# A deeper convolution pipeline in the head and four staggered lanes in the tail of a scan kernel

## The chip, the cores and the metric

The kernel runs on one core of one Trainium2 chip. The metric is the device time of one execution in microseconds (us). Each kernel was run several times and profiled once. Every run told here is of the fast state. A difference counts as faster or slower from 2% up; below that the verdict is "same", and smaller effects are read from stages of the profile.

Engines: PE is the matrix engine TensorE (PEld its weight loads), DVE is VectorE, ACT is ScalarE, POOL is GpSimd, SP is the engine that issues most DMAs; "SPq" is a DMA issue in SP's queue.

## The reference, cut to what matters

Four images of 64 × 64 × 96 go through one block (projection, convolution, selective scan in four directions) and then one layer of linear attention and a feed-forward net.

```python
xz = bilinear(x, W_in, s_in, b_in)              # sign(x) @ sign(W).T * scale
xp, z = jnp.split(xz, 2, axis=-1)
t = conv3x3(sign(xp + move0_b), sign(conv_W) * mean|conv_W|)
t = prelu(t + conv_b + rp_b0) + rp_b1 + xp
u = silu(t)                                      # 192 channels, 4096 points
# four directions: rows, columns, and both reversed
dts, Bs, Cs = split(bilinear(u in the direction, Wl, ...))
h = exp(delta * A) * h + delta * u * B           # 16 states per channel, step by step
y = sum(h * C) + D * u
# ... the four directions summed, layer norm, gate silu(z), projection; then
# attention (one 96 x 96 matrix per image, known only once all of it is summed), FFN
```

## The kernel before

The program has three stages. The **head** makes the weights' signs, convolves the first image in 16 parts, forms B, C and delta ("row stage", "start"). The **scan** runs 1536 pieces and takes the other images' heads along. The **tail** finishes the last image in lanes: sums and norms (three lanes), the 96 × 96 matrix ("middle"), the rest (`last`, four lanes).

Work is written as generators; `interleave` advances each by one step and so sets the order in every engine's queue. The instructions of an engine run in that order in these traces: in part 2 below, u is ready at 67.7 us and starts at 74.4, behind two casts in DVE's queue.

```python
def run(c):                                     # head
    made, first = c.weights(), prologue(c, 0, c.xts)
    ...
    while (0, 1) not in c.ready:
        interleave([made, first])               # one weights step, one prologue step
        c.later.tick()                          # stores that are due go to SP

# convolution, one part, two deep: matmuls of part n, all else of part n-1
for s in range(4):
    ...4 or 3 matmuls of part n into cv; the projection ahead at s = 0 and 2...
    if prev:
        if s == 0: cz = cz*s + v; cz = cz + r*oma          # DVE twice
        elif s == 1: sign(...); e = exp(-cz)               # ACT twice
        elif s == 2: e = ln(1+e); e = exp(-e)              # ACT twice
        elif s == 3: u = cz*e; store u; by_columns(u)      # DVE, SP; POOL turns it
v = cv*acs + acb                                           # DVE
r = relu(cv*csc + cbias)                                   # ACT, same bank
cz = winT.T @ xsT                                          # PE

def sign(h, q, pz):
    ...
    for m in range(3):
        c.later.store(xgw[...], sg[m::3, :])               # SP

# scan.start(): loads of utd and bc are issued here
nc.sync.dma_start(v[0], ud[0:128, 0:16])                   # 512 KB of utd first
for q in range(NQ):
    self.load_bc(0, self.bt, 0, 0, 0, q)                   # then 2 MB of bc
for x in range(2): ...                                     # then 256 KB of utd

# tail
drain([e.middle()])
drain([e.last(ln) for ln in [e.lane] + more])              # four lanes in lockstep
```

Here sg, v, r, e and u take turns on eight tiles of one pool, five tiles to a part: a tile is free for its next owner only when the store that reads it has landed. (... cut: everything of the scan, and the branches for images after the first.)

## Time and profile before

5479.21 us in the median of its first runs, 5478.45 over those of the comparison with the change. The stages are cut at visible events of the timeline: first convolution matmul, last sign, first copy of the row stage, first and last scan, first matmul with the finished matrix.

| stage of before | from | to | us |
|---|---|---|---|
| weights and projection | 0 | 56.2 | 56.2 |
| convolution to its last sign | 56.2 | 173.5 | 117.3 |
| hand-over to the row stage | 173.5 | 188.3 | 14.8 |
| row stage | 188.3 | 211.1 | 22.9 |
| delta and the first loads | 211.1 | 237.7 | 26.6 |
| scan | 237.7 | 5355.5 | 5117.8 |
| tail up to the matrix | 5355.5 | 5407.5 | 52.0 |
| `last` in four lanes | 5407.5 | 5482.3 | 74.8 |

The lines that carry this reading stand in the prediction. The table is for the time between two events on different engines, which no single view prints: take both starts from the timeline and subtract.

### The profile page before, as it was taken

The numbers are of one execution on the slowest core, as the hardware profiler recorded it, in microseconds if no ns is written. First come the engines' busy times: TensorE is split into PE (matmuls) and PEld (weight loads), VectorE is DVE, ScalarE is ACT, GpSimd is POOL, SyncE is SP. The second block draws the span as 40 slices with busy tenths as digits, with TensorE's granted clock in tenths as the row PEclk, the third lists the DMA queues.
The fourth block names the chain that finished last, engine by engine and source line by source line (L and its number), as shares of the span: only waits on it lengthen the run. The fifth ranks groups of instructions, "written<-read, shape, count | busy, mean of one in ns | idle before, by whom it ended". The sixth has DMA issues, their size and how long they took to land. (4 is left out here: it accounts for less than half of the span.)

```text
span 5482.3 us, 62080 instructions
## 1 busy us (share of the span) xinstructions
PE 3415.9 (62%) x20083; PEld 1355.4 (25%) x20083; DVE 5016.3 (91%) x3171; ACT 3615.3 (66%) x5648; POOL 4938.7 (90%) x2245
## 2 busy tenths in 40 slices
PE   6456665467656776657764676664676664444577
PEld 3222222122222222222222222221232221111233
DVE  4499999899999999999999999999999999999994
ACT  4467777687766667778777666776666775555554
POOL 2399999899999999999999999999999999999990
PEclk7666776678766777767886787766787666666777
DMA  4565666767666666576665665667666565665652
GB/s 82 128 211 171 207 207 199 228 213 213 195 200 201 189 208 204 196 244 213 217 199 181 216 198 186 216 192 225 217 218 187 189 204 194 195 211 194 212 175 62
DMA packets 624219, 1069.06 MB, mean 195 GB/s; under 512 B 237307, under 2 KB 355092, under 8 KB 622100
## 3 DMA queue, kind: packets, MB, share of 16 engines
q1 hardware_dynamic: 623236, 1065.07, 62.2%
q8 instruction: 157, 2.57, 0.2%
q14 instruction: 170, 1.39, 0.1%
q10 hardware_dynamic: 656, 0.02, 0.0%
HBM read 830.01 MB, written 228.56 MB: 193 GB/s over the span
## 5 line engine op out<-in xcount | busy, mean ns | idle before, releaser
L423 POOL TENSOR_TENSOR w<-dl,bc 128x1024 f32<-128x1024 f32 x1524 | 3550.0, 2355 | 88.0 <-PE yp L1462 52.8
L1389 ACT ACTIVATE dA<-dl,anm 128x1024 f32<-128x1024 f32 x1524 | 1701.1, 1116 | 486.0 <-DVE w L423 284.5
L423 DVE TENSOR_TENSOR_SCAN dA<-dA,cy,w 128x1024 f32<-128x1024 f32 x725 | 1698.6, 2343 | 107.8 <-ACT dA L1389 94.2
L423 POOL TENSOR_TENSOR w<-h,bc 128x1024 f32<-128x1024 f32 x570 | 1341.4, 2353 | 127.8 <-DVE h L423 113.6
L1462 PE MATMUL yp<-w,sum 128*32 128x256 f32 x12288 | 1254.7, 505 | 323.8 <-ACT pd L1343 235.0
L423 DVE TENSOR_TENSOR w<-dA,bc 128x1024 f32<-128x1024 f32 x966 | 1183.1, 1225 | 65.4 <-DMA bc<-bcd 4.0
L423 DVE TENSOR_TENSOR_SCAN h<-dA,cy,w 128x1024 f32<-128x1024 f32 x427 | 999.2, 2340 | 17.4 <-ACT dA L1389 16.7
L1462 PEld LDWEIGHTS yp<-w,sum 128*32 128x32 f32 x12288 | 316.9, 127 | 1401.0 <-issue 731.4
L1431 ACT COPY cy<-dA 128x1 f32<-128x1 f32 x725 | 114.0, 157 | 753.2 <-DVE w L423 751.3
L423 DVE TENSOR_TENSOR_SCAN dA<-dA,w 128x1024 f32<-128x1024 f32 x241 | 550.2, 2283 | 34.7 <-ACT dA L1389 28.0
L1324 PE MATMUL dps<-gT,wdz 128*128 128x64 fp8e5 x1008 | 116.6, 316 | 399.9 <-ACT ys L1476 373.9
L423 DVE TENSOR_TENSOR_SCAN h<-dA,w 128x1024 f32<-128x1024 f32 x143 | 325.9, 2279 | 18.8 <-POOL w L423 16.1
L1337 PE MATMUL dps<-sp,ident 128*128 128x512 f32 x378 | 268.5, 799 | 96.2 <-ACT dps L1333 96.1
L1467 PE MATMUL yp<-ya,back 128*128 128x256 f32 x576 | 226.3, 511 | 0.0
L682 PE MATMUL cv<-tp,cwA 128*96 128x512 fp8e5 x576 | 197.9, 467 | 33.3 <-ACT r L729 30.9
L1324 PEld LDWEIGHTS <-wdz 128*128 128x128 fp8e5 x1008 | 95.6, 153 | 479.2 <-issue 451.7
L1324 PE MATMUL dps<-gT,wdy 128*128 128x64 fp8e5 x504 | 58.7, 318 | 221.0 <-ACT ys L1476 220.8
L1431 ACT COPY cy<-h 128x1 f32<-128x1 f32 x427 | 79.3, 186 | 133.5 <-DVE h L423 132.8
L994 PE MATMUL yc<-eys,mean 96*96 96x512 f32 x240 | 141.4, 744 | 29.5 <-DVE vks L423 14.4
L1329 ACT ACTIVATE pd<-dps,dbias,pvd 128x512 f32<-128x512 f32 x189 | 143.9, 761 | 20.8 <-PE dps L1324 20.5
L1467 PEld LDWEIGHTS yp<-ya,back 128*128 128x128 f32 x576 | 117.6, 236 | 119.9 <-issue 88.2
L1330 ACT ACTIVATE sp<-dps,dbias,pvd 128x512 f32<-128x512 f32 x189 | 144.8, 766 | 0.0
(363 smaller groups left out, 4457.2 us busy)
## 6 DMA issues: line engine op xcount, KB each, us to landing
dl<-dld SPq DMA_DIRECT2D x762, 512.0 KB
bc<-bcd SPq DMA_DIRECT2D x512, 512.0 KB
dld<-pd SPq DMA_DIRECT2D x126, 512.0 KB
yd<-ys SPq DMA_DIRECT2D x768, 64.0 KB
dld<-pd SPq DMA_DIRECT2D x126, 256.0 KB
ya<-yd SPq DMA_DIRECT2D x192, 128.0 KB
pu<-ud SPq DMA_DIRECT2D x32, 512.0 KB
pu<-utd SPq DMA_DIRECT2D x31, 512.0 KB
```

Source lines behind the costliest of these rows:

```text
L423: return getattr(self.eng, name)(out, *args, **kw)
L682: nc.tensor.matmul(ps, w[:, 96 * h : 96 * h + 96], tp[:, 8 * q + dy : 8 * q + dy + 8, dx : dx + IW], start=(w is taps[0][1]), stop=(w is t ...
L994: self.c.nc.tensor.matmul(ps, w, x, start=(i == 0), stop=(i == len(pairs) - 1))
L1324: nc.tensor.matmul(pv[:, s], wd[:, k, s], gT[:, :, c0 : c0 + 16], start=(s == 0), stop=(s == 7))
L1329: nc.scalar.activation(d[:, 0], ps, AF.Abs, scale=sc, bias=bi)
L1330: nc.scalar.activation(t, ps, AF.Relu, scale=sc, bias=bi)
L1337: nc.tensor.matmul(ps, c.ident, t, start=False, stop=True, skip_group_check=True)
L1389: c.nc.scalar.activation(t, self.dlt[i // NQ][0], AF.Exp, scale=c.anm[:, g, NQ * KORD[e] + q : NQ * KORD[e] + q + 1])
L1431: self.c.nc.scalar.copy(self.carries[g, q], h[:, CH - 1 : CH])
L1462: c.nc.tensor.matmul(y[32 * x : 32 * x + 32, g % 2, :], c.sum4, prod[:, 256 * x : 256 * x + 256], start=(q == 0), stop=(q == NQ - 1 and no ...
L1467: c.nc.tensor.matmul(y[:, g % 2, :], w, src, start=False, stop=(n == len(more) - 1))
```

## The change

Its intent: keep all engines busy in the convolution by working on three parts at once, take away waits for memory and for DMA around it, and let the four lanes of the tail use different engines at the same time. The diff, cut to its core (pool names, the weights' `scales` block, the reversed order in which the tail takes its columns, and unchanged branches left out):

```diff
+    next(made)
     while (0, 1) not in c.ready:
-        interleave(lanes)
+        interleave([first])                    # weights only every second step
         c.later.tick()
+        if (0, 1) not in c.ready:
+            interleave(lanes)
+            c.later.tick()
...
-                per = 2 if alone and h else 4  # u turned: 64- or 128-byte runs
+                per = 2 if alone else 4        # 64-byte runs, tiles of the scan's pool
...
+                    if alone and q == NQ8 - 1:
+                        held.append((dst, ut)) # last two stores after the last part
-                    c.later.store(xgw[...], sg[m::3, :])
+                    if alone:
+                        nc.gpsimd.dma_start(dst, sg[m::3, :])
...
+            def alone_parts():                 # conv n, sign/exp n-1, Ln/Exp/u n-2
...
+                if fast and j % 4 > 1:         # row stage: four banks
+                    return c.p.ps.tile([128, 512], F32, ..., tag=f"y{j % 2}")
...
                     nc.sync.dma_start(gw[:, x, 16:64], ...sgd...)
+                    if fast and x:
+                        c.loads_ahead()        # bc x4, then utd
...
+        if i == len(self.pieces) - 1:
+            self.last_ys = t                   # last y read from its tile
+            return
...
+    last = [e.last(ln) for ln in [e.lane] + more]
+    for g in last:
+        next(g)                                # first loads ahead of the matrix
     drain([e.middle()])
-    drain([e.last(ln) for ln in [e.lane] + more])
+    drain([apart(2 * x, g) for x, g in enumerate(last)])
```

## The prediction

> **What bounds the kernel now.** I read the page's busy row and its 40 slices first, then a table of windows with edges at visible events (start of the convolution, the first row-stage copy, the first scan, the last scan), then the waits of the first 240 us, the timeline of one convolution part, and the chain that ended last.
>
> The page, busy row and two slices:
>
> ```profile
> PE 3415.9 (62%) x20083; PEld 1355.4 (25%) x20083; DVE 5016.3 (91%) x3171; ACT 3615.3 (66%) x5648; POOL 4938.7 (90%) x2245
> ...
> DVE  4499999899999999999999999999999999999994
> ...
> POOL 2399999899999999999999999999999999999990
> ```
>
> DVE and POOL are full in slices 3 to 39 and half idle in the first two and the last. The windows say so with times (start:end, length, busy of PE, PEld, DVE, ACT, POOL, PE clock, DMA share, GB/s):
>
> ```profile
> 13.00:41.50 28.50, 12.83 (x62) 8.08 (x61) 13.96 (x34) 11.03 (x27) 12.42 (x39) 0.53 0.70 86
> ...
> 77.00:110.00 33.00, 23.44 (x93) 11.78 (x92) 12.39 (x17) 22.13 (x36) 4.23 (x4) 0.95 0.52 67
> 110.00:145.00 35.00, 26.98 (x96) 13.16 (x95) 14.56 (x20) 22.51 (x36) 5.29 (x5) 0.85 0.47 87
> ...
> 177.00:188.00 11.00, 1.05 (x8) 0.93 (x9) 0.00 (x0) 0.00 (x0) 0.81 (x1) 0.50 0.73 102
> ...
> 237.70:5350.00 5112.30, 3183.78 (x19064) 1237.10 (x19065) 4864.77 (x2903) 3442.40 (x5363) 4890.02 (x2131) 0.72 0.64 203
> ...
> 5405.00:5482.00 77.00, 58.79 (x195) 24.97 (x194) 37.97 (x73) 38.69 (x65) 0.00 (x0) 0.74 0.22 62
> ```
>
> So there are three stages: a head of 237.7 us, a scan of about 5119 us at 95% of DVE and 96% of POOL, and a tail of about 125 us. The change hardly touches the scan's instructions. At most 363 us are therefore open to it, and 2% of the whole is 109.6 us: nearly a third of head and tail together.
>
> The waits of the head show a serial chain rather than a busy engine:
>
> ```profile
> DVE u L423 <- ACT e L713: 54.5, 15, 4.6
> ACT r L729 <- DVE v L726: 29.7, 16, 4.3
> ...
> PE xa L760 <- DMA xg<-sg: 15.3, 1, 15.3
> ACT xr L765 <- DMA utd<-ut: 12.3, 1, 12.3
> ```
>
> One part of the convolution, from the timeline (only the starts matter): v 104.32, r 105.15, second multiply-add 106.08, sign 106.91, exp 107.40, tp 107.88, sz 108.54, Ln 109.21, Exp 109.87, u 110.53, next v 111.14. That is 6.82 us in which DVE and ACT take turns. The fourth row above is a buffer: the row copies reuse memory of the u tiles, so they wait until the stores of u have landed, at 188.25, although the matmul they read had started at 181.97.
>
> The tail's chain walks all four lanes through each operation together (start, us):
>
> ```profile
> 5408.83 5.98 DMA l4t<-td
> 5414.94 1.99 PE l4ps L994 x2
> ...
> 5430.35 0.70 DVE h L1218
> 5431.08 0.36 DVE h L1219
> 5431.46 0.43 DVE h L1220
> ```
>
> First DMA alone, then PE alone, then ACT alone, then DVE alone from 5430 to 5437.
>
> **What the Trainium skill says.** (1) "TensorE: Matmul & The Clock Gate", Part 1 (the HAM clock gate): TensorE runs at 1.2 GHz until about 3.4 us of sustained work have passed, then at 2.4; a 512-column matmul starts every 426.7 ns cold and every 215.7 ns warm. The trace agrees: weight loads of the convolution are 0.43 us apart near 105, and six of its matmuls near 110.7 take 1.46 us; the window 77 to 110 has clock 0.95, 177 to 213 has 0.50. (2) "PSUM — Partial Sum Buffer", "PSUM bank collisions raise a hardware error": engines have to be kept out of one bank and quadrant at once, readers too. The trace agrees in form: r waits for v 16 times, 29.7 us, though both only read cv. (3) "DMA: Bandwidth & Descriptors", "Issuing engines are not separate DMA queues": issuing from another engine saves only sequencer time. The same page's specifications give a first byte of about 1 us from GpSimd against 0.6 from SP. The page of before has no queue of GpSimd's, so no run yet shows it; three SP issues of sg take 1.77 us in the timeline.
>
> **The change part by part.**
>
> *Weights ahead of and inside the convolution.* Before, everything of the weights is made by 56.1. The window 13 to 41.5 has DVE 14, ACT 11, POOL 12.4, PE 12.8 of 28.5 us busy, with a 9.0 us wait of the first projection matmul for xb behind DVE's reduces. The change moves those reduces behind it, interleaves weights with the eight xb/project steps, and starts the convolution with 15 weight steps to come. The reduces' wait (about 8) and the stretch after the projects (41.6 to 56.1, of which half stays) give 15: convolution from 41. Given back: 8 fp8 transposes and casts at about 1.2 us on DVE (10), some small DVE work (5), and two POOL items of 4.1, over parts 0 to 5.
>
> *Three parts deep.* A part then costs its busiest engine, not the 6.82 chain. ACT by issue intervals: sign 0.49, exp 0.48, Ln 0.66, Exp 0.66, r 0.66, tp 0.66 (1.33 where it comes in two halves), sz 0.67: 4.28 to 4.95 with the next image row's projection, 2.95 without. DVE: v 0.80, two multiply-adds 1.5, u 0.69: 3.0, plus weights 2.5 in parts 0 to 5. PE: 18 matmuls by 0.22 = 4.0 warm, or by 0.43 = 7.7 cold. I take 6.5 for six parts (DVE with weights, order of queues), 4.7 for six, 3.7 for four and 6.5 for draining: 39+28+15+6.5 = 88.5, last sign at 129.5, against 173.5. Cumulative gain 44, of which 15 from the start and 29 from the parts (56.1 to 173.5 was 117.4).
>
> *sg by GpSimd, u tiles in a memory of their own.* xa waited for the last xg store, 8.4 us after the last sign (181.94 to 173.53); SP was held by issues of ud (6.02 at 172.84). From the otherwise idle GpSimd I expect sign + 5.5, less 3. The copies then come at once instead of 6.3 us after xa. Together 8.5: first row copy at about 135.7, cumulative 52.5.
>
> *Four row banks.* Before, 188.25 to 196.03 for xa/xb in two banks at a 1.37 pace for two n, PE's eight matmuls 1.01 of it. I expect −1.6; of the accumulation (pace 2.84, PE 1.98 of it) −2.0, limited because tbc and sgn (0.83 each) stay serial in a bank. Cumulative 56.1.
>
> *Loads ahead of the matrix.* bc and utd loads (2.8 MB) go out 3.6 us earlier. In 213 to 237.7 the DMA moved 223 GB/s, share 0.74, and the dl_s load took 8.15 us behind them. I credit 2.5. First scan: 237.7 − 58.6 = about 179.
>
> *Scan.* Nothing removed; it shifts as a block. Taken as 0, with ±5 for buffer timing.
>
> *Last y from tile to tile.* Removes four stores of ys (5367.3 to 5369.1) and a trip through DRAM before loads that ln0 and ln1 waited for until 5375.1 and 5377.7. The data come about 5 us earlier, but PE handles lanes in order and lane 0 is not released earlier: 2.
>
> *Loads ahead of the middle.* The td loads went out from 5404.73 behind m0 and landed lane by lane: matmuls at 5407.45, 5410.13, 5412.65, 5414.94. Now they start at about 5400.6. The transfers then run beside the middle, but only the first q is needed: I credit 1.3.
>
> *Lanes two steps apart.* Eight q remain per core. The last 74 us hold PE 58.8, DVE 38.0, ACT 38.7 busy. Of PE much is at the cold rate: a q needs three fp32 matmuls of 0.86 in total pairs, hp 0.65, fy 0.65 and ft 1.22, about 5.1 warm, so 41 for eight. A q has about 13 steps and the lanes begin two apart: 2×13 + 3×2 = 32 rounds. With four different operations in one round, on three engines, a round costs about 1.75 us, the larger of an ACT and a DVE item plus a semaphore hop: 56 against 72 now. I credit 15. Tail in all: −18.
>
> Sum: −15 −29 −8.5 −3.6 −2.5 −18 = −76.6 us, 5479.2 − 76.6 = 5402.6. I round up to 5405 since small terms seldom all arrive.
>
> **Rivals.** *A: TensorE stays cold.* If DVE's weight casts leave gaps, PE falls to 0.43 per matmul, a part costs at least 7.7, and the convolution's 29 us vanish: about 5434. For it: clock 0.69 in 56 to 77. Against: 0.95 right after, with the same eighteen matmuls per 6.8 us; a denser stage should be warmer. *B: GpSimd becomes the part's bound.* It gets three DMA issues a part, the ut copy of 1.06, and weights work; its cost per issue is not in this trace. At 1 us each (the estimate of the skill's first-byte figure) a part has 4.1 on POOL, just under ACT. At 2 us it is 7 and the gain goes: 5425 to 5432. *C: the moved weights cost more inside than they did ahead*, because each DVE item there delays a v or u and ACT behind it: parts 0 to 5 at 8 instead of 6.5, 9 us lost: 5414. *D: DMA collides.* The utd stores of 64-byte runs (6144 packets; the one issued at 180.81 landed at about 188.25) are held until after the last part and then stand ahead of bcd and sgd stores, and SP stood 16 us at the anm transfers (76 to 92): 5 to 10 us back, 5410 to 5415. *E: lanes apart gives little*, since PE serves them in order and its clock drops when its work is thinned: tail −5 instead of −18, 5418. *F, upward: ACT's bound is reached in all parts*, and the lanes come close to PE's 41: another 20, 5385.
>
> **Range and chances.** A or B whole is 1 in 8 together; C, D and E in part are likely, F in part too. Predicted 5405 us, eight in ten between 5380 and 5436. Faster by over 2% needs below 5369.6, that is 33 us beyond my sum: 0.06. Within 2%: 0.93. Slower: 0.01, since it would need the scan to lose over 100 us.
>
> **What would show it.** Right: convolution begins near 41, first scan near 179, r's waits for v and u's for e mostly gone, xr no longer waiting for utd; parts 6 to 11 paced by ACT at about 4.7; last scan to end about 105 instead of 126 us; the scan from first to last scan within 5 us of before. Wrong: clock near 0.5 in the convolution (A); POOL or a GpSimd issue as releaser of sg's tiles or of xa (B); v or u waiting in DVE's order behind weight casts (C); sgn's store or dl_s landing late (D); the tail's rounds at 2.2 us or more (E); or a scan stage that changes by more than 10 us, which I have no term for.

## The result, and the profile after

The changed kernel took 5450.82 us in the median (5443.04 to 5457.05, four runs) against 5478.45. Ratios here are the mean time of one kernel's fast runs over that of the other's of the same rounds, so not quite the ratio of the medians: 0.995, with a 95% interval of 0.9933 to 0.9967. By the 2% rule that is "same", but clearly faster by 28 us. Predicted were 5405 us and a gain of 74, with 5380 to 5436 as range: the time lies outside.

The profiled executions differ by 38.2 us (5482.3 to 5444.1), more than the medians, because before's profiled run (5484 us) was one of its longest and after's (5446 us) one of its shorter. Stage by stage:

| stage | before | after | difference | predicted |
|---|---|---|---|---|
| start to last sign | 173.5 | 159.6 | −13.9 | −44 |
| hand-over to row stage | 14.8 | 4.3 | −10.5 | −8.5 |
| row stage | 22.9 | 18.2 | −4.7 | −3.6 |
| delta and first loads | 26.6 | 29.2 | +2.6 | −2.5 |
| scan | 5117.8 | 5113.1 | −4.7 | 0 |
| tail up to the matrix | 52.0 | 49.8 | −2.2 | −3.3 |
| `last` | 74.8 | 69.9 | −4.9 | −15 |
| sum | | | −38.3 | −76.9 |

(The predicted column adds 0.3 more than the prediction's −76.6, which rounded the tail.) Two lines are short: the convolution by 30 us and `last` by 10. One has the wrong sign.

The page's busy row and the slices of DVE and POOL, which answer to the first lines of the prediction:

```profile
PE 3394.4 (62%) x20083; PEld 1348.6 (25%) x20083; DVE 5015.2 (92%) x3171; ACT 3614.2 (66%) x5648; POOL 4962.0 (91%) x2293
...
DVE  4599999899999999999999999999999999999995
...
POOL 3599999899999999999999999999999999999990
```

The scan is as full as before; the second slice is a little fuller. POOL has 48 instructions more, the issues of sg's stores.

The convolution next. The waits of the first 240 us of the changed kernel, where before had u waiting for e (54.5 us) and r waiting for v (29.7):

```profile
POOL xg L701 <- ACT sg L693: 60.0, 16, 13.7
...
ACT r L751 <- DVE v L750: 24.0, 8, 5.8
...
PE cz L753 <- DVE u L435: 18.9, 7, 11.1
```

The serial chain is gone, as predicted: u's wait for e is no longer among the long ones. GpSimd's wait for sg is idle time of a free engine and costs nothing. PE's wait for u is the same delay seen from the matmul cz, which takes turns on two banks with the cz that u reads. But r still waits 24 us for v, in 8 parts instead of 16. Where, the signs tell. Their starts in the 16 parts are 62.5, 68.9, 79.9, 87.8, 95.9, 101.5, 106.6, 110.8, 115.9, 121.4, 134.6, 139.7, 145.2, 150.5, 154.5, 159.6. Parts 6 to 9 take 4.2 to 5.5 us, near the 4.7 of the prediction. Part 2 takes 11.0, parts 3 and 4 take 8, part 10 takes 13.2, and the last ones take 4 to 5.5 where 3.7 was expected.

The timeline through part 2:

```profile
67.08 0.63 ACT L730 ACTIVATE e<-e 96x512 f32<-96x512 f32 x1
...
68.43 1.17 PE L199 MATMUL tps<-identb,slab 128*128 128x128 bf16 x8 [2.03 <-ACT tp L624]
...
69.64 1.22 DVE L201 CAST wdy<-tps 128x1024 fp8e5<-128x1024 bf16 x1 [2.20 <-PE tps L199]
...
73.25 1.23 DVE L201 CAST wdy<-tps 128x1024 fp8e5<-128x1024 bf16 x1 [2.39 <-PE tps L199]
74.40 0.68 DVE L435 TENSOR_TENSOR u<-cz,e 96x512 f32<-96x512 f32 x1
...
75.83 0.77 ACT L751 ACTIVATE r<-cv,cbias,csc 96x512 f32<-96x512 f32 x1 [5.83 <-DVE v L750]
```

The input of u is ready at 67.7. But ahead of u in DVE's queue stand two casts of weights (wdy), and each waits for its transposes in PE's queue, which stand among the convolution's matmuls. So u starts at 74.4, v behind it, and r has waited 5.83 us.

The timeline through part 10:

```profile
109.73 16.57 SPq L397 DMA_DIRECT2D anm<-in_al  x24
...
126.40 1.52 SPq L454 DMA_DIRECT2D ud<-u  x3
...
128.81 0.59 ACT L738 ACTIVATE e<-cz 96x512 f32<-96x512 f32 x1 [6.81 <-DMA ud<-u]
...
129.52 0.81 DVE L750 TENSOR_SCALAR v<-cv,acs,acb 96x512 f32<-96x512 f32 x1 [8.61 <-DMA ud<-u]
```

The 24 loads of anm occupy SP for 16.6 us. Three stores of u stand behind them, so their tiles are not given back, and e and v find no tile. In the kernel before the same 16 us lay at 76 to 92 and cost nothing that its signs show, probably because each part took 7 us anyway and the tiles were needed later.

The windows put the last parts down to DMA (columns as in the prediction: PE, PEld, DVE, ACT, POOL busy, clock, DMA share, GB/s):

```profile
62.00:102.00 40.00, 29.60 (x166) 16.09 (x166) 25.33 (x55) 24.31 (x41) 19.89 (x53) 0.91 0.28 54
102.00:125.00 23.00, 20.21 (x85) 10.74 (x84) 11.67 (x16) 18.50 (x31) 12.69 (x20) 0.93 0.43 26
125.00:160.00 35.00, 17.36 (x70) 8.99 (x68) 17.21 (x24) 19.54 (x33) 12.67 (x20) 0.82 0.88 137
```

From 125 to 160 no engine is over 56% busy, and the DMA share is 0.88. SP's queue is as full: its issues fill 30.7 of these 35 us (sum of SP's timeline). The clock is above 0.8 in all three rows, so the cold TensorE of rival A is not the cause.

In the start of the scan, DVE waits for a load that the prediction counted as brought forward:

```profile
185.76 2.50 SPq L1451 DMA_DIRECT2D bc<-bcd  x4
188.31 0.72 SPq L1590 DMA_DIRECT2D w_u<-utd  x1
...
198.03 0.69 DVE L435 TENSOR_TENSOR w_s<-w_s,w_u 128x512 f32<-128x512 f32 x1 [2.61 <-DMA w_u<-utd]
```

It was brought forward in time, but put behind 2 MB of bc.

The tail from 6 to 36 us into `last`:

```profile
5380.00:5386.00 6.00, 4.91 (x7) 1.23 (x6) 1.28 (x2) 2.40 (x5) 0.00 (x0) 0.50 0.20 63
5386.00:5392.00 6.00, 5.65 (x8) 1.41 (x7) 2.64 (x5) 2.53 (x4) 0.00 (x0) 0.50 0.11 31
5392.00:5398.00 6.00, 5.65 (x9) 1.51 (x7) 2.95 (x7) 3.73 (x6) 0.00 (x0) 0.50 0.00 2
5398.00:5404.00 6.00, 5.49 (x23) 2.80 (x22) 3.75 (x9) 3.91 (x7) 0.00 (x0) 0.78 0.11 33
5404.00:5410.00 6.00, 5.21 (x26) 2.67 (x24) 5.85 (x12) 5.21 (x9) 0.00 (x0) 1.00 0.12 34
```

TensorE is 94% busy from 5386 to 5398, at clock 0.50: one pair of fp32 matmuls takes 2.02 us there, 0.86 in the prediction's count.

### The profile page after: what moved, and what is told of

Read it like the earlier page. It is cut to its first block, busy times and chain, and to the rows that moved or that the text cites. A ratio compares the mean times of both kernels' runs of the same rounds, so it can differ in the third digit from the quotient of the medians.

```text
span 5444.1 us, 62119 instructions
## 1 busy us (share of the span) xinstructions
PE 3394.4 (62%) x20083; PEld 1348.6 (25%) x20083; DVE 5015.2 (92%) x3171; ACT 3614.2 (66%) x5648; POOL 4962.0 (91%) x2293
## 5 line engine op out<-in xcount | busy, mean ns | idle before, releaser
L773 PE MATMUL cv<-tp,cwA 128*96 128x512 fp8e5 x432 | 156.4, 482 | 30.2 <-ACT r L805 27.7
```

The costliest lines, as they stand in the source:

```text
L773: nc.tensor.matmul(ps, w[:, 96 * h : 96 * h + 96], tp[:, 8 * q + dy : 8 * q + dy + 8, dx : dx + IW], start=(w is taps[0][1]), stop=(w is t ...
```

## The experiments

The theory after this first look: (T1) weights woven into the convolution hold u and v in the in-order queues; (T2) many tiny DMA packets hold the DMA engines and through them the tiles; (T3) the order of the loads ahead cost the start 2.6 us; (T4) the tail's first round is bound by TensorE at half clock. Rivals stand with each run. Diffs are against the changed kernel; "last sign" and "first scan" were 159.6 and 211.3 us there.

### The same kernel again

> The changed kernel unaltered, to see how far its stages repeat. If its four runs of 5443 to 5457 us are one kernel in two moods, the head (first scan at 211.3 us) and the tail (69.9 us from the first matmul with the matrix to the end) repeat within 1 us and a difference of some 10 us sits in the scan stage (5113.1 us in the first profile). Rival: the head itself is unsteady, and the first scan moves by 5 us or more.

No edit. Median 5448.89 us, ratio 0.9952 (0.9937 to 0.9967). Last sign 159.1, first scan 210.6, scan 5113.2, `last` 69.9: the head and the stages repeat within 1 us in a profile. Its runs still spread from 5445.55 to 5456.19. Neither guess on the spread was decided by this profile; later ones give part of it: `last` took 74.7 us instead of 70 in three kernels whose tail is unaltered (anm_spread, ut_contig, both_dma), and the scan, unaltered in all, took 5110.9 to 5119.6. So a difference of 5 us in a total says little here. In late_loads and two_banks, whose convolutions are unaltered, the last sign came at 163.3 and 162.5, so the head too moves by up to 4 us. Lengths of stages after it repeat better.

The two lengths of `last` go with TensorE's clock. Its long stretch at half clock was 23.9 us in the changed kernel's profile and 37.6 in anm_spread's, with the same tail; these two windows lie inside them (the first of the changed kernel, the second of anm_spread):

```profile
5376.80:5400.40 23.60, 21.12 (x28) 5.65 (x28) 8.07 (x15) 9.84 (x16) 0.00 (x0) 0.50 0.25 72
...
5377.00:5414.40 37.40, 34.92 (x70) 13.93 (x69) 16.17 (x31) 17.67 (x29) 0.00 (x0) 0.50 0.15 44
```

So 13.7 us more at half clock went with 4.8 us more time, and a change of the tail has to gain more than that in one profile to be seen.

### anm's loads spread out

> The 24 loads of anm, issued in one run of 16.6 us on SP in the convolution, are spread by fours over six weight steps. Theory: behind them the stores of u stand in SP's queue, their tiles do not come free, and so part 10 takes 13.2 us; then it falls to about 5.5, the last sign comes at about 151 instead of 159.6, and the first scan at about 203 instead of 211.3. Rival: the DMA engines, not SP's queue, are held by these loads' tiny packets; then the delay only spreads over neighbouring parts and the last sign stays within 2 us of 159.6.

```diff
             for j in range(4):
                 nc.sync.dma_start(anm[j::4, g, :], src[j])
+            yield
```

Median 5453.14 us, ratio 0.996 (0.9946 to 0.9974). Last sign 159.4, first scan 211.2. The rival holds: part 10's stall of 13.2 us became two of 9.1 and 9.7 (at signs 120.0 and 134.4). Breaking up the run of issues alone gives nothing; my expectation of 8 us was wrong. That the DMA engines and not SP's queue are held, the rival's reason, isn't shown by it: SP still has the same issues to make in the convolution.

### utd before bc

> Only the order of the loads ahead is changed: utd (768 KB) before the four bc loads (2 MB), as in the kernel before. Theory: the loads came earlier but utd last, so DVE waited 2.6 us for it; then the product of delta and u ends some 2.5 us earlier and the first scan at about 208.8 instead of 211.3. Rival: the DMA is the bound of this stretch in any order; then dl_s lands no earlier and the first scan stays at 211 within 1 us.

```diff
-        for q in range(NQ):
-            self.load_bc(0, self.bt, 0, 0, 0, q)
         self.first_us = [...]
         ...
         for x in range(2):
             nc.sync.dma_start(v[1][64 * x : ...], ud[...])
+        for q in range(NQ):
+            self.load_bc(0, self.bt, 0, 0, 0, q)
```

Median 5448.00 us, ratio 0.9948 (0.9933 to 0.9963). First scan at 208.3, 3.0 us earlier, with the last sign at 159.9. From the first gp matmul to the first scan it takes 22.8 us, against 25.5 in the changed kernel and 22.9 before. T3 holds, and with it: the loads ahead are worth nothing in the right order and cost 2.6 in the wrong one.

### Large packets for the turned u tiles

> Wrong result on purpose: each store of a turned u tile writes 4 KB runs instead of 64-byte runs, same bytes. Theory: these packets hold the DMA engines (share 0.91 from 140 to 160 us) and delay the release of tiles and the stores of bcd; then parts 11 to 15 fall from 5.1 to about 4.2 us each, tbc of the second half waits 3 instead of 5.9 us, and the first scan comes 7 to 10 us earlier, about 203. Rival: these parts are bound by the order of ACT and DVE; then the signs stay at 5.1 us apart and the first scan moves by under 3 us.

```diff
-                    dst = c.utd[b][h].rearrange("p (w h) -> p w h", h=IH)[:, :, rows]
+                    dst = c.utd[b][h][:, CH * (q // 2) : CH * (q // 2) + CH].rearrange("p (w h) -> p w h", w=IW)
```

Median 5442.26 us, ratio 0.9937 (0.9922 to 0.9952). The data of two directions are in the wrong order here, although the comparison with the reference still passed: it is too loose to see this, and passing it is weak evidence for any of these variants. Last sign 153.0, first scan 203.8, 7.5 us earlier, as expected. After a stall of 12.2 us at anm the parts run at 3.5 to 5.0 us. T2 gains: same bytes, fewer packets, and the last parts are as fast as the prediction had them. But large packets relieve two things at once. The issue that SP makes right after a store of utd took 4.8 to 6.5 us in the changed kernel and 0.3 to 0.7 here (the first two lines are of the changed kernel, the others of this run):

```profile
128.01 0.61 SPq L454 DMA_DIRECT2D utd<-ut  x1
128.72 5.25 SPq L454 DMA_DIRECT2D ud<-u  x1
...
125.39 0.38 SPq L454 DMA_DIRECT2D utd<-ut  x1
125.85 0.40 SPq L454 DMA_DIRECT2D ud<-u  x1
```

From 125 to the last sign SP issues for 6.7 of 28 us here, 30.7 of 35 in the changed kernel. So the small packets are the cost, but whether they hold the tiles by way of the DMA engines, as T2 says, or of SP's queue, this run can't tell (sg_sp below bears on it).

### Both DMA loads lightened

> Both DMA loads of the convolution are lightened: anm spread as in the run before, and the turned u tiles stored in 4 KB runs (wrong result on purpose). Alone the first moved the last sign by 0 us, the second by 6.6, with one stall of 12 us left at anm. Theory, that the small packets hold the DMA engines and these hold the tiles: without both, no part after the sixth takes over 5.5 us and the last sign comes at about 143 to 146, the first scan at about 195. Rival, that SP's queue has a fixed amount of issuing to do and anm's 16 us are part of it: the last sign stays at 150 or later.

The two edits above together. Median 5440.29 us, ratio 0.9929 (0.991 to 0.9947). Last sign 147.4, first scan 198.6, near the better end of what was expected (one part still took 8.2). Spreading anm, worth nothing alone, is worth 5.6 us once the u tiles' packets are out of the way, and the two together are worth 12.2. A fixed amount of issuing in SP's queue would have kept the last sign at 150 or later. The amount wasn't fixed, though, since large packets shorten SP's issues too. T2 holds as far as the packets go; the path from them to the tiles it doesn't show.

### Weights advanced every step

> The weights lane is advanced every step, so almost all weights are made before the convolution, as in the kernel before; the rest of the change stays. Theory (moving them paid): the convolution starts later, parts 0 to 5 fall from 7 or 8 to about 5 us each, and the last sign comes 2 to 8 us later than 159.6. Rival C of the prediction (moved weights cost more inside than ahead): the last sign comes 3 us or more earlier than 159.6.

```diff
     while (0, 1) not in c.ready:
-        interleave([first])
+        interleave(lanes)
         c.later.tick()
-        if (0, 1) not in c.ready:
-            interleave(lanes)
-            c.later.tick()
```

Median 5438.56 us, ratio 0.9932 (0.9918 to 0.9947). The first convolution matmul comes at 60.0, 12 us later, and the last sign at 150.8, 8.8 us earlier. The theory of the expectation (that moving weights in paid) falls and rival C stands: parts 1 to 5 take 23.8 us from first to sixth sign, 39.0 in the changed kernel, which is 7.8 a part where C had 8. DVE's work on weights there is only some 10 us (an estimate: 25.3 busy from 62 to 102, less 3.0 for each of five parts), so some 5 of the 15.2 us lost go beyond the moved work itself.

But this edit moves more than the casts. The loads of anm are a step of the weights too, and SP now issues them before the convolution:

```profile
51.52 16.26 SPq L397 DMA_DIRECT2D anm<-in_al  x24
```

At the sixth sign (97.7 against 101.5) the gain is 3.8; the other 5.0 come later, where the changed kernel has its stall at anm. So 8.8 is the price of all weight steps in the convolution, anm's issues included, and that it lies near C's 9 is luck. The window of six parts:

```profile
74.00:100.00 26.00, 21.50 (x96) 11.50 (x95) 15.03 (x25) 23.41 (x39) 13.29 (x22) 1.00 0.42 80
```

ACT is 90% busy in it, against 61% from 62 to 102 in the changed kernel: this is the ACT bound that the deeper pipeline was to reach.

### The memsets first

> The three memsets of the convolution's padded tiles move to the start of GpSimd's queue. In the changed kernel the first sign of the projection waits for them until 41.2 us behind weights' copies on GpSimd, though its matmul ended at 31.1. Theory: the convolution's first matmul comes at about 42 instead of 48.0 and the last sign 4 to 6 us earlier. Rival: the scales on DVE (v needs them, done at 34.4) and the transposes that stand in PE's queue before part 0 set the start, or the DMA of later parts takes the gain back; then the last sign moves by under 2 us.

```diff
             sub = ExitStack()
+            if alone:
+                nc.gpsimd.memset(xgw[64:128, 1], 0.0)
+                for h in range(2):
+                    nc.gpsimd.memset(tflat[h].bitcast(F32), 0.0)
```

(and the same three taken out further down for the first image). Median 5445.57 us, ratio 0.9941 (0.9926 to 0.9956). The convolution starts at 43.0 instead of 48.0, and the last sign comes at 157.7, only 1.9 earlier, which is less than the 4.2 us over which that event scatters (159.1 to 163.3 with unaltered convolutions). The rival holds: an earlier start is taken back by what binds later.

### All three costs of the convolution gone

> Wrong result on purpose (4 KB runs for the turned u tiles): weights first, anm early, large packets, so that all three suspected costs of the convolution are gone. Theory: every part then costs about 4 to 5 us with projections ahead and 3.6 after, so from the first v to the last sign takes about 70 us (101.8 in the changed kernel, 82.0 with weights first), which is what the prediction had assumed for parts 6 to 15. Rival: something else paces the parts too (order of the queues, PE's clock) and it takes over 77 us.

```diff
 (as weights_first and ut_contig, and)
-        for g in range(NG): ... anm loads at the end of weights()
+        for g in range(NG): ... anm loads behind the weights' own loads
```

Wrong on purpose as ut_contig is. Median 5426.58 us, ratio 0.9905 (0.989 to 0.992). Last sign 138.6. From the first v (68.9) to the last sign it took 69.7 us, 101.8 in the changed kernel. That is the 70 that was expected. The last sign is 12.2 us earlier than with weights first (150.8) and 21.0 earlier than in the changed kernel. That 8.8 and the 12.2 of both_dma make just 21.0 is partly chance, as each of these two runs moves or spreads anm's loads. So the size of a part without these costs was rightly estimated; what was left out were the costs.

### sg's stores back on SP

> The xg stores of sg go back from GpSimd's queue to SP's. Theory: SP's queue and the DMA engines are loaded in the convolution, so the tiles of sg come free later and xa waits for the last of them: last sign 2 to 8 us later than 159.6, the first row copy 6 or more after the last sign instead of 4.3, the first scan at about 216 to 221. Rival B (GpSimd's issues are themselves a burden): the last sign comes earlier or stays within 1.5 us, and only the transition to the row copies gets longer.

```diff
-                    if alone:
+                    if False:
                         nc.gpsimd.dma_start(dst, sg[m::3, :])
```

Median 5460.19 us, ratio 0.9968 (0.9956 to 0.998). Last sign 173.0, first scan 228.3: 17 us later, more than any expectation. One part takes 23 us, and the hand-over takes 6.8 instead of 4.3:

```profile
110.80 16.29 SPq L397 DMA_DIRECT2D anm<-in_al  x24
127.19 0.57 SPq L454 DMA_DIRECT2D ud<-u  x1
127.85 1.85 SPq L454 DMA_DIRECT2D xg<-sg  x3
```

With sg's stores behind anm too, more tiles are held. From the waits of this run:

```profile
DVE u L435 <- DMA ud<-u: 20.2, 2, 19.1
```

One u waited 19.1 us for an earlier store of u to land. The bytes stored are the same here and only the queue differs, so SP's queue is at least one path by which tiles are held; how much the DMA engines add stays open. Rival B falls, and of all parts of the change tested here, giving the stores to GpSimd is worth most.

### Two banks in the row stage

> The row stage goes back to two PSUM banks. From the first row copy to the end of the last sgn took 18.2 us in the changed kernel, 22.9 before. Theory: the four banks are worth about 3.5 us, so it takes about 21.5 and the first scan comes at about 214.5. Rival: the second half waits for the store of bcd (5.9 us) whatever the banks, and part of the gain is taken back there: under 2 us.

```diff
-                if fast and j % 4 > 1:
+                if False and j % 4 > 1:
```

Median 5454.36 us, ratio 0.996 (0.9946 to 0.9974). From the first row copy to the end of the last sgn 22.3 us against 18.2: four banks are worth 4.1, near the 3.6 predicted. The wait for the store of bcd (4.0 here, 5.90 with four banks) takes some of it back, as the rival said, though the gain is twice its 2 us:

```profile
172.43 1.58 SPq L906 DMA_DIRECT2D bcd<-tbc  x1
...
178.30 2.96 DVE L874 TENSOR_SCALAR tbc<-acc,sbR 128x512 f32<-128x512 f32 x4 [5.90 <-DMA bcd<-tbc]
```

This is the changed kernel: the store went out at 172.43 and landed at 178.3, while the two held utd stores had been issued from 163.2 to 168.9. With large packets for these (ut_contig) the stage took 17.2 us instead of 18.2, so their packets hold up at most a small part of it.

### The lanes in lockstep

> Only the lanes of the last stage are put back to one step, 0 apart instead of 2; loads ahead stay. From the first matmul with the matrix to the end took 69.9 us with them apart (74.7 in two of the profiled runs), 74.8 in the kernel before. Theory (being apart is worth little, as TensorE runs at half clock through the thin first 24 us): 70 to 75 us. Rival (prediction: 15 us saved): over 82 us, since the loads ahead hid only 1 or 2.

```diff
-    drain([apart(2 * x, g) for x, g in enumerate(last)])
+    drain([apart(0 * x, g) for x, g in enumerate(last)])
```

Median 5452.43 us, ratio 0.9955 (0.994 to 0.9969). `last` takes 73.6 us, 69.9 with lanes apart in most profiles and 74.7 in three. So these profiles put the stagger at 3.7 us, or at nothing where the clock was as low as in those three; 15 it is not.

### The loads behind the middle

> The first loads of the last stage go back behind the middle. From the last scan to the first matmul with the matrix took 49.8 us in the changed kernel. Theory (the prediction's: worth about 1.3 us): the first matmul comes 1 to 2.5 us later after the last scan, 51 to 52, and the later lanes, two steps apart, do not notice, so from there to the end stays at 70 or 75. Rival: the lanes also wait for data one by one as in the kernel before, and the end comes 5 us later.

```diff
-    for g in last:
-        next(g)
     drain([e.middle()])
+    for g in last:
+        next(g)
```

Median 5448.18 us, ratio 0.9947 (0.9934 to 0.9961). From the last scan to the first matmul with the matrix 49.7 us, 49.8 with loads ahead; `last` 70.0 against 69.9. The loads ahead are worth nothing, below both guesses. What is left of the 2.2 us before the matrix is then the last y taken from its tile, 2 in the prediction; I didn't undo that part by itself.

### Lanes one step apart

> Lanes one step apart instead of two. Theory (TensorE at half clock through the first round is what ate the gain): less spread means fewer single-lane steps at the start, TensorE gets its clock earlier and the stage takes 66 to 70 us. Rival (spread itself is what pays, and more is better): between the 73.6 of lockstep and the 69.9 of two apart, 71 to 72.5.

```diff
-    drain([apart(2 * x, g) for x, g in enumerate(last)])
+    drain([apart(x, g) for x, g in enumerate(last)])
```

Median 5445.31 us, ratio 0.9942 (0.9928 to 0.9955). `last` took 66.5 us, less than with 0 (73.6) or 2 (69.9). In the first 20 us of the stage the clock was now 0.83 and 1.00. This fits T4, and that more spread is better isn't borne out. But it is one profile, the 3.4 us are less than the 4.8 between two profiles of one tail, and here the clock fell to 0.50 again for the last 19.7 us.

### A cheaper variance matmul

> The variance matmul of the last stage takes bf16 squares (result a little less exact), so that TensorE has about 0.64 us less per q warm and 1.4 to 1.6 us less cold; nothing else changes. Theory (in the stage's first round TensorE at half clock is the bound, 94% busy): it shortens by at least 5 us, from 69.9 to 62 to 65. Rival (it is bound by the chain of ACT and DVE, TensorE's busy time being padded by its slow clock): it shortens by under 2.5 us, as only each lane's own chain gets shorter.

```diff
             t = f32("fq")[0:96]
+            if self.alone:
+                t = t.bitcast(BF16)[:, 0:512]
             nc.scalar.activation(t, pc, AF.Square)
-            mm(ps, [(c.on96, t)])
+            mm(ps, [(c.on96h if self.alone else c.on96, t)])
```

Median 5443.61 us, ratio 0.9941 (0.9927 to 0.9954). `last` takes 63.6 us, 6.3 less, with no step or wait taken out. T4 holds: less TensorE work shortens the stage by more than the rival's 2.5, and the last version below repeats it (63.7). TensorE was still at 0.50 from 2.4 to 22.9 us into the stage, and in these ten us of it 93% busy:

```profile
5391.00:5401.00 10.00, 9.29 (x14) 2.81 (x14) 5.94 (x12) 6.50 (x11) 0.00 (x0) 0.50 0.07 22
```

Why the clock stays at half with the engine so busy is left open: late and early rise were both seen in kernels with the same tail.

### Versions meant to beat both

> A version meant to beat both: weights advanced every step (last sign 8.8 us earlier alone), anm's loads issued early among the weights' loads, utd before bc (3.0 us earlier alone), memsets first. If the costs add, the last sign comes at about 145 instead of 159.6, the first scan at about 194 to 198 instead of 211.3, and the time at about 5432. Rival: anm's 16 us of issuing ahead only move the stall to the stores of xb and the start of the convolution; then the first scan is at 200 to 203, as with weights first alone.

weights_first, utd_first and early_memset together, with anm's loads early. Median 5439.26 us, ratio 0.9933 (0.9918 to 0.9948). First scan 200.7, last sign 152.0: the rival's range. The early anm and memsets add nothing, since with weights advanced every step anm's issues lay before the convolution already (from 51.5 us); what beats weights_first in the first scan (203.1) is the order of loads.

> A version meant to beat both with a right result: weights advanced every step (first scan 8 us earlier alone), utd before bc (3 us alone), variance matmul of the last stage in bf16. If they add: first scan at 200, stage after the matrix 63 to 65, time about 5431 to 5435. If the bf16 step does nothing: about 5438.

weights_first, utd_first and fv_bf16. Five rounds: median 5428.41 us (5422.17 to 5434.80), ratio 0.9911 (0.9897 to 0.9925), which lies apart from the changed kernel's 0.9952 (0.9937 to 0.9967). First scan 201.0, `last` 63.7. The gains nearly add (200 was expected at the first scan), and the version beats both kernels, with the bf16 squares as its price in exactness.

## Why the prediction was wrong

**What bounds the kernel.** Right: head and tail hold all of the gain; the scan shifts as a block, and its −4.7 us lies in the spread of the unaltered scan (5110.9 to 5119.6).

**Three parts deep.** This is the step that failed: "A part then costs its busiest engine, not the 6.82 chain". The chain did go, and without weights and small packets a part costs what was said (69.7 us from first v to last sign). But the sum took only the engines as bounds. It left out that DMA gives the tiles back: large packets and a spread anm bring the last sign 12.2 us forward. And it took 6.5 for a part with weights (2.5 us of DVE for them), while waiting in order made it 7.8; made ahead, weights and anm together cost 8.8 less. Where the 30.1 us went can be read at the signs, if part 0 and the draining (13.0 predicted) are put ahead of the first:

| stretch | predicted | measured | missing |
|---|---|---|---|
| start | 41 | 48.0 | 7.0 |
| to the first sign | 13.0 | 14.5 | 1.5 |
| parts 1 to 5, with weights | 32.5 | 39.0 | 6.5 |
| parts 6 to 11, with anm | 28.2 | 38.2 | 10.0 |
| parts 12 to 15 | 14.8 | 19.9 | 5.1 |

So half of it lies in parts 6 to 15, where the tiles came back late. Both causes were named, D with 5 to 10 us and C with 9, and called likely in part; yet the sum was rounded by only 2.4 us for all of them. They came together. Three parts share the same eight tiles as two did; more tiles, an obvious other cure, were not tried.

**Weights ahead.** 15 us credited, 8.2 measured at the first matmul (48.0 for 56.2); of the 7 missing, 5.0 were the memsets in GpSimd's queue. The early memset shows that most of even such a gain vanishes by the last sign.

**sg by GpSimd and u tiles.** 8.5 credited, 10.5 in the hand-over; undoing only the queue costs 17 at the first scan. Rival B wrong: three issues take 1.47 us of GpSimd (at 69.81 in the changed kernel's timeline). B's estimate of 1 us for each, a first-byte figure, was twice that.

**Row banks.** 3.6 credited, 4.7 measured from stage to stage, 4.1 by undoing it.

**Loads ahead.** 2.5 credited; measured nothing in the right order (22.8 us from gp to scan, 22.9 before) and a loss of 2.6 in the order it had. The error: I read the DMA as one queue to start sooner, without asking which load in it DVE needs first.

**Tail.** Last y: 2 credited, about 2.2 seen. Loads ahead of the middle: 1.3 credited, 0.1 measured. Lanes apart: 15 credited, 3.7 to 4.9 measured, and nothing in the profiles with the long stretch at half clock. (Two readings were off: the window called the last 74 us is 77 long, and the 72 of now are 74.8.) The failing term is "a round costs about 1.75 us": it took TensorE's warm pace (5.1 us per q), while the first round ran cold with pairs of 2.02 us; 69.9 us over its 32 rounds are 2.2 a round. Rival E had this, with −5 for −18; measured −7.1.

Sum: in the profiles 38.6 us are missing (76.9 − 38.3). The convolution is 30.1 short, the tail 11.2, the start 5.1; hand-over, row stage and scan gave 2.0, 1.1 and 4.7 more. The rest of the 46 between 5405 and 5451 is the choice of profiled runs (38.2 against 27.6 in the medians), less what I had rounded up.

## What to carry to other kernels

When a pipeline gets deeper, count its tiles and ask what gives each back: a store in a queue, behind which loads, in packets of what size. Work moved from a quiet stage into a busy one can cost more than its busy time, since others wait behind it in in-order queues, so measure it against making it ahead. When several loads are moved forward together, the one that is consumed first goes first. And look at the clock of every profile before two of them are compared.

## What the Trainium skill lacked or had wrong

- "TensorE: Matmul & The Clock Gate", Part 1: about 3.4 us of sustained work are said to bring the full clock. In the tail of the changed kernel TensorE stayed at 0.50 from 5376.8 to 5400.4 us, 89% busy, and in anm_spread, with the same tail, from 5377.0 to 5414.4, 93% busy; there `last` took 4.8 us longer. What counts as sustained for pairs of fp32 matmuls with gaps of 0.3 to 0.8 us isn't told.
- "DMA: Bandwidth & Descriptors", "Issuing engines are not separate DMA queues": issuing elsewhere is said to save only sequencer time, usually small. Here 48 issues moved from SP to GpSimd were worth 17 us at the first scan, since on SP they stood behind 16.3 us of other issues and held tiles.
- "DMA: Bandwidth & Descriptors", "Why small descriptors are slow (HBM only)": the direction agrees; the page's example is a descriptor of 256 bytes, with 27% overhead. The same bytes in 4 KB runs instead of 64-byte ones brought the first scan 7.5 us forward, and 12.7 with anm spread as well; the issue next in SP's queue took 0.3 to 0.7 us instead of 4.8 to 6.5.
- No page that I read says what an in-order queue costs when independent streams are woven together; here five parts of the convolution took 15.2 us longer, for some 10 us of DVE work.
